# Two 3x3 convolutions by minimal filtering on rows, and a final stage with more buffers

## The chip, the core and the metric

The kernel runs on one core of a Trainium2 chip. The metric is the device time of one execution in microseconds. Before the change it is 2103.16 us (median of three runs, 2087.83 to 2104.97); the profiled execution spans 2096.1 us. Five engines work side by side, each through its own instructions in order: TensorE (PE, with its weight loads as PEld), VectorE (DVE), ScalarE (ACT), GpSimd (POOL), and SyncE (SP), which here issues most DMA transfers.

## What is computed

Two "metaformer" layers on x of shape (2, 256, 56, 56). Layer 0 mixes by 7x7 window attention and then a mixture of eight experts of which each token uses two; layer 1 mixes by two 3x3 convolutions and then another mixture of experts. The change lies in layer 1's convolutions, in what leads into them, and in the last step.

```python
def noised_tri_conv(x, w):
    tw = w - jnp.mean(w)
    tq = ternary_quantize(tw)                 # -1, 0 or 1 by thirds of the range
    out = conv3x3(x, tq)                      # padding 1
    return out + einsum('bchw,oc->bohw', x, tq[:, :, 1, 1])
...
out1 = relu(batch_norm_train(noised_tri_conv(x, w1), g1, b1))
out2 = batch_norm_train(noised_tri_conv(out1, w2), g2, b2)
return relu(out1 + out2)
...
t = t + moe_0(ln(t)); x = x_of(t)
x = x + conv_layer(ln(x)); t = tokens_of(x)
t = t + moe_1(ln(t))
```

The extra term doubles the middle tap, so one convolution with weights of -1, 0, 1 (middle tap -2, 0, 2) gives the whole. The batch norm needs the mean and variance over both images before its first output.

## The kernel before

**Data.** The two images are cut into 14 strips of 8 rows and 56 columns (448 positions); the 256 channels are two halves of 128 partitions (`KC = 2`). `pad[b]` holds one padded image, `X[b, s]` what a convolution gives for one strip, and `XT[b, s]` is the same memory seen as 112 tokens x 4 x 256.

**Order of the stages.** Attention and routing of layer 0; its experts (56 tiles of 256 rows, lines 940 to 1016), which scatter results to `ys`; the two convolutions (`combine`, `split`, `conv`, `affine`, `between`, lines 1532 to 1617); residual, norm and routing of layer 1; its experts; and the final stage (lines 1702 to 1714). In the expert and routing stages the written order is kept on each engine. In the convolutions and the final stage a planner, working from its own idea of costs, orders each engine's instructions; on the chip each engine then keeps that order.

**Weights of the convolutions.** `ternary` (line 1431) makes the quantised weights `wq1` and `wq2` in small steps on VectorE: three reductions for each of nine parts, then three comparisons for each. Two such steps follow each tile of the first experts (`beside`).

**Into the first convolution.** `combine(i)` (line 1532) loads a strip's tokens (`x_on`) and its two expert results per token (`got`, 896 KB, from `ys`, two buffers), adds them with eight multiply-adds on VectorE (line 1058), normalises (`token_norm`, with VectorE doing the scaling, line 1074), turns the strip by TensorE transposes (line 1089), and ScalarE copies it into `pad` (line 1539).

**A convolution.** For each strip, `split` makes two parts of ten rows of `pad`: `hi`, rounded for the fast matmul type (ScalarE, line 1551), and the rest `lo` (VectorE, line 1552), each in two buffers. Then for each output half, 2 input halves x 9 taps x 2 parts = 36 matmuls of 448 columns add into one PSUM block:

```python
for k in range(KC):
    for t in range(TAPS):
        dy, dx = divmod(t, 3)
        for part in (hi, lo):
            nc.tensor.matmul(pc[:, :NT], wq[:, k, t, o * P : (o + 1) * P],
                             part[:, k, dy : dy + SR, dx : dx + W], ...)
```

ScalarE copies the block to `X` (line 1583) and VectorE takes its statistics (line 1584). Between the convolutions `affine` makes scale and shift, and `between` writes the Relu of the scaled result into `pad` on ScalarE (line 1607). GpSimd has nothing to do in either convolution.

**The final stage.** For each strip `gather` loads `got`, adds it to `XT` by eight multiply-adds on VectorE, TensorE turns it, ScalarE copies it to `o_out`, and SyncE stores it. `got` and `o_out` have two buffers each. SyncE issues both loads and stores, in one order.

Of the kernel before, what the change touches and what calls it, by code (L numbers as in the profile page):

```python
# [10 lines left out]
F32 = mybir.dt.float32  # L11
F32R = mybir.dt.float32r
# [8 lines left out]
P = 128  # L21
B, C, H, W = 2, 256, 56, 56
KC = C // P
# [37 lines left out]
TAPS = 9  # L61
NW = C * C * TAPS
# [557 lines left out]
def metaformer(ctx: ExitStack, tc: tile.TileContext, a: dict, out: bass.AP, flag):  # L620
# [427 lines left out]
    def gather(i, ys, wgt, tp, xt):  # L1048

        rows = NTT * TOP * TT  # L1050
        y = tp.tile([TT, NTT, TOP, C], F32, tag="got", name="got")
        nc.sync.dma_start(
            y, ys[i * rows : (i + 1) * rows, :].rearrange("(p t j) c -> p t j c", t=NTT, j=TOP)
        )
        for t in range(NTT):
            n = i * NTT + t
            for j in range(TOP):
                nc.vector.scalar_tensor_tensor(
                    xt[:, t, :], y[:, t, j, :], wgt[:, j, n : n + 1], xt[:, t, :], ALU.mult, ALU.add
                )  # L1060

    def token_norm(tp, xt, eps):
        stats = tp.tile([TT, NTT, 6], F32, tag="t_stats", name="t_stats")
        mv = tp.tile([TT, NTT, 2], F32, tag="t_mv", name="t_mv")
        for t in range(NTT):
            nc.vector.bn_stats(stats[:, t, :], xt[:, t, :])
        for t in range(NTT):
            nc.vector.bn_aggr(mv[:, t, :], stats[:, t, :])
        rstd = tp.tile([TT, NTT], F32, tag="t_rstd", name="t_rstd")
        nc.scalar.activation(rstd, mv[:, :, 1], AF.Sqrt, bias=eps[:TT])  # L1070
        nc.vector.reciprocal(rstd, rstd)
        xn = tp.tile([TT, NTT, C], F32, tag="xn", name="xn")
        for t in range(NTT):
            nc.vector.tensor_scalar(
                xn[:, t, :],
                xt[:, t, :],
                mv[:, t, 0:1],
                rstd[:, t : t + 1],
                ALU.subtract,
                ALU.mult,  # L1080
            )
        return xn
# [17 lines left out]
    def finish(steps):  # L1100
        for _ in steps:
            pass
# [306 lines left out]
    for b, s in STRIPS:  # L1409
        XT[b, s] = xpool.tile([P, NTT, C], F32, tag=f"x{b}_{s}", name=f"x{b}_{s}")  # L1410
        X[b, s] = XT[b, s].rearrange("p t c -> p (t c)")[:, : KC * NT].rearrange(
            "p (k n) -> p k n", n=NT
        )

    with ExitStack() as mid:
# [15 lines left out]
        def ternary(name, wq, ps_pool, tag, tp, held):  # L1431
# [5 lines left out]
            bufs = [t.rearrange("p t c -> p (t c)") for t in held]  # L1437
            wqf = wq.rearrange("p k t c -> p (k t c)")
            parts = [(n, bufs[n // wide][:, n % wide : n % wide + PART]) for n in range(0, size, PART)]

            def load(i):
                n = min(wide, size - i * wide)
                nc.sync.dma_start(bufs[i][:, :n], a[name + "_flat"][:, i * wide : i * wide + n])
# [40 lines left out]
            for n, part in parts:  # L1484
                low = tp.tile([P, PART], F32, tag="low", name="low", bufs=1)
                nc.vector.tensor_scalar(low, part, mean, lo, ALU.subtract, ALU.is_lt)
                yield
                nc.vector.tensor_scalar(part, part, mean, hi, ALU.subtract, ALU.is_gt)
                yield
                nc.vector.tensor_tensor(wqf[:, n : n + PART], part, low, ALU.subtract)  # L1490
                yield
            middle = wq[:, :, TAPS // 2, :]
            nc.vector.tensor_scalar_mul(middle, middle.bitcast(F32), 2.0)
# [3 lines left out]
        wq1 = wqp.tile([P, KC, TAPS, C], F32R, tag="wq1", name="wq1")  # L1497
        wq2 = wqp.tile([P, KC, TAPS, C], F32R, tag="wq2", name="wq2")

        with ExitStack() as st:  # L1500
# [4 lines left out]
            def prepare():  # L1505
                half = len(STRIPS) // 2
                held = [XT[s] for s in STRIPS]
                yield from ternary("L1_conv_w1", wq1, ps, "pt", tp, held[:half])
                yield from ternary("L1_conv_w2", wq2, ps, "pt", tp, held[half:])
# [3 lines left out]
            def beside(j):  # L1513
                for _ in range(2):
                    next(steps, None)
# [6 lines left out]
        with ExitStack() as st:  # L1522
            rp = st.enter_context(tc.tile_pool(name="raw", bufs=1, reuse_waits="tile"))
            tp = st.enter_context(tc.tile_pool(name="conv_t", bufs=2, reuse_waits="tile"))
            ps = st.enter_context(tc.tile_pool(name="conv_ps", bufs=4, space=PSUM, reuse_waits="tile"))

# [5 lines left out]
            def combine(i):  # L1532
                xt = tp.tile([TT, NTT, C], F32, tag="x_on", name="x_on")
                nc.sync.dma_start(xt, x_mid[i])
                gather(i, ys[0], wgt0, tp, xt)
                xn = token_norm(tp, xt, eps6)
# [8 lines left out]
            def split(i):  # L1545

                b, s = STRIPS[i]
                rows = pad[b][:, :, s * SR : s * SR + SR + 2, :]
                hi = tp.tile([P, KC, SR + 2, WC], F32R, tag="hi", name="hi")
                lo = tp.tile([P, KC, SR + 2, WC], F32R, tag="lo", name="lo")  # L1550
                nc.scalar.copy(hi, rows)  # L1551
                nc.vector.tensor_tensor(lo, rows, hi.bitcast(F32), ALU.subtract)  # L1552
                return hi, lo

            def conv(wq, ahead):

                stats = rp.tile([P, KC, len(STRIPS), 6], F32, tag="stats", name="stats")
                ahead(0)
                ahead(1)
                parts = [split(0)]  # L1560
                for i, (b, s) in enumerate(STRIPS):
                    if i + 2 < len(STRIPS):
                        ahead(i + 2)
                    if i + 1 < len(STRIPS):
                        parts.append(split(i + 1))
                    r = X[b, s]
                    hi, lo = parts.pop(0)
                    for o in range(KC):
                        pc = ps.tile([P, 512], F32, tag="cv", name="pc")
                        n = 0  # L1570
                        for k in range(KC):
                            for t in range(TAPS):
                                dy, dx = divmod(t, 3)
                                for part in (hi, lo):
                                    nc.tensor.matmul(  # L1575
                                        pc[:, :NT],
                                        wq[:, k, t, o * P : (o + 1) * P],
                                        part[:, k, dy : dy + SR, dx : dx + W],
                                        start=n == 0,
                                        stop=n == 2 * KC * TAPS - 1,  # L1580
                                    )
                                    n += 1
                        nc.scalar.copy(r[:, o, :], pc[:, :NT])  # L1583
                        nc.vector.bn_stats(stats[:, o, i, :], r[:, o, :])  # L1584
# [16 lines left out]
            stats = conv(wq1, combine)  # L1601
# [13 lines left out]
            stats = conv(wq2, between)  # L1615
# [85 lines left out]
    with ExitStack() as st:  # L1701
        tp = st.enter_context(tc.tile_pool(name="last_t", bufs=2, reuse_waits="tile"))
        ps = st.enter_context(tc.tile_pool(name="last_ps", bufs=2, space=PSUM, reuse_waits="tile"))
        for i, (b, s) in enumerate(STRIPS):
            xt = XT[b, s][:TT]
            gather(i, ys[1], wgt1, tp, xt)
            pu = channels(ps, "pu", xt)
            o = tp.tile([P, KC, NT], F32, tag="out", name="o_out")
# [5 lines left out]
            nc.sync.dma_start(x_out[b, :, :, s * NT : (s + 1) * NT], o)  # L1714
# [116 lines left out]
```

## Time and profile before

| stage | from, us | to, us | length |
|---|---|---|---|
| attention, routing, wait for the first tile | 0 | 673.5 | 673.5 |
| experts of layer 0 | 673.5 | 901.6 | 228.1 |
| until the first convolution's first matmul | 901.6 | 929.9 | 28.3 |
| first convolution | 929.9 | 1154.2 | 224.3 |
| between | 1154.2 | 1161.6 | 7.4 |
| second convolution | 1161.6 | 1376.7 | 215.1 |
| residual and routing of layer 1 | 1376.7 | 1598.3 | 221.6 |
| experts of layer 1 | 1598.3 | 2010.2 | 411.9 |
| final stage | 2010.2 | 2096.1 | 85.9 |

The borders are first and last matmuls of a kind. Over the whole span TensorE is busy 84%, VectorE 39%, ScalarE 31%, GpSimd 28%. A busy TensorE says little by itself, since a matmul's record lasts longer than the distance to the next one; what a matmul costs is that distance. The waits are to be read stage by stage: an engine that is idle in a stage which another one fills costs nothing there.

### The profile page before, as it was taken

To read this page: it belongs to the slowest core of one execution; us is meant where nothing else is said; L and a number is where in the kernel's file an instruction comes from. 1 tells how busy PE (TensorE), PEld (TensorE's weight loads), DVE (VectorE), ACT (ScalarE), POOL (GpSimd) and SP (SyncE) were. 2 spreads that over 40 slices of the span, in tenths; PEclk is the share of its full clock that TensorE was granted. 3 is DMA by queue.
4 is the path that set the end of the run, shared out by engine and by line. 5 is a ranking of instruction groups with operands and counts; after the bars stand their busy time and mean duration, and the time that the engine had idled before them with its cause. 6 is when DMAs were issued, how large, how long until landed. Compare 5 with 4: busy or idle time off the path is not lost. (4 is left out here: it accounts for less than half of the span.)

```text
span 2096.1 us, 27450 instructions
## 1 busy us (share of the span) xinstructions
PE 1750.4 (84%) x9656; PEld 1394.0 (67%) x9656; DVE 819.1 (39%) x2538; ACT 645.6 (31%) x1227; POOL 586.0 (28%) x677
## 2 busy tenths in 40 slices
PE   3999799898882999959999899966435999999953
PEld 1565466464561888848888788855424888888842
DVE  4355345253452656568531111156541111111135
ACT  1444334343241333322211411134312333333311
POOL 4023544334424444510000000015562222222210
PEclk9999899898775999979999999965557999999975
DMA  3000221111114989876310000013325666666647
GB/s 85 28 27 28 63 80 44 55 32 54 59 43 164 316 267 339 287 198 200 97 35 1 0 1 1 1 54 105 99 81 202 230 229 228 229 231 235 224 142 237
DMA packets 77329, 263.48 MB, mean 126 GB/s; under 512 B 16150, under 2 KB 21242, under 8 KB 66880
## 3 DMA queue, kind: packets, MB, share of 16 engines
q1 hardware_dynamic: 55680, 209.83, 31.6%
q0 software_dynamic: 21504, 51.82, 7.1%
q8 instruction: 78, 1.28, 0.3%
q14 instruction: 67, 0.55, 0.1%
HBM read 190.53 MB, written 74.72 MB: 127 GB/s over the span
## 5 line engine op out<-in xcount | busy, mean ns | idle before, releaser
L833 POOL DMA_INDIRECT xs<-u,pos x224 | 215.4, 962 | 623.6 <-ACT ut L748 496.4
L1575 PE MATMUL pc<-hi,wq 128*128 128x448 f32 x1008 | 379.1, 377 | 9.7 <-ACT hi L1551 9.7
L1575 PE MATMUL pc<-lo,wq 128*128 128x448 f32 x1008 | 377.6, 375 | 0.6 <-DVE lo L1552 0.6
L1016 POOL DMA_INDIRECT ys<-y,to x224 | 220.4, 984 | 449.7 <-DVE dest L969 293.3
L990 PE MATMUL ph<-ut,w 128*128 128x256 f32 x1344 | 311.6, 382 | 2.3 <-DMA w<-in_L_experts 2.3
L1006 PE MATMUL py<-w,h 128*128 128x256 f32 x1344 | 308.1, 379 | 1.2 <-DVE y L1014 1.2
L1006 PEld LDWEIGHTS py<-w,h 128*128 128x128 f32 x1344 | 255.3, 190 | 36.2 <-ACT h L997 1.5
L990 PEld LDWEIGHTS ph<-ut,w 128*128 128x128 f32 x1344 | 248.6, 192 | 33.1 <-issue 2.9
L1014 DVE TENSOR_TENSOR y<-py,w 128x512 f32<-128x512 f32 x112 | 77.5, 692 | 426.3 <-PE py L1006 303.8
L1575 PEld LDWEIGHTS pc<-hi,wq 128*128 128x128 f32 x1008 | 192.0, 191 | 32.3 <-ACT hi L1551 10.5
L1575 PEld LDWEIGHTS pc<-lo,wq 128*128 128x128 f32 x1008 | 191.7, 190 | 23.3 <-DVE lo L1552 1.8
L997 ACT ACTIVATE h<-ph,w 128x256 f32<-128x256 f32 x336 | 159.1, 473 | 122.4 <-PE ph L990 97.5
L1257 ACT ACTIVATE ex<-sc 112x476 f32<-112x476 f32 (+3 forms) x224 | 116.8, 571 | 238.9 <-PE sc L1247 188.6
L966 ACT COPY ut<-pt 128x512 f32<-128x512 f32 x112 | 65.6, 586 | 332.3 <-PE pt L962 326.7
L1275 DVE TENSOR_TENSOR acc<-av,acc 128x238 f32<-128x238 f32 (+3 forms) x224 | 89.5, 408 | 168.2 <-PE av L1267 109.3
L1267 PE MATMUL av<-ex,vals 112*64 112x238 f32 (+3 forms) x896 | 127.9, 409 | 7.5 <-DVE acc L1275 5.9
L962 PE MATMUL pt<-ident,xg 128*128 128x128 f32 x448 | 68.8, 278 | 71.8 <-DMA xg<-xs 71.8
L1238 PE MATMUL sc<-q_im,keys 32*112 32x238 f32 (+3 forms) x896 | 108.5, 439 | 20.6 <-issue 15.5
L962 PEld LDWEIGHTS pt<-ident,xg 128*128 128x128 f32 x448 | 57.2, 144 | 82.6 <-DMA xg<-xs 42.1
L1584 DVE BATCH_NORM_STATS2 stats<-x 128x6 f32<-128x448 f32 x56 | 35.0, 625 | 179.1 <-ACT x L1583 178.8
L1583 ACT COPY x<-pc 128x448 f32<-128x448 f32 x56 | 29.7, 531 | 226.2 <-PE pc L1575 226.2
L1267 PEld LDWEIGHTS av<-ex,vals 112*64 112x64 f32 x896 | 58.0, 146 | 59.4 <-issue 32.2
(211 smaller groups left out, 2072.8 us busy)
## 6 DMA issues: line engine op xcount, KB each, us to landing
w<-in_L_experts SPq DMA_DIRECT2D x56, 1154.0 KB
w<-in_L_experts SPq DMA_DIRECT2D x56, 641.0 KB
xg<-xs SPq DMA_DIRECT2D x112, 260.0 KB
got<-ys SPq DMA_DIRECT2D x28, 896.0 KB
xt<-in_x_tok SPq DMA_DIRECT2D x14, 448.0 KB
xr<-in_x_tok SPq DMA_DIRECT2D x14, 448.0 KB
x_mid<-xr SPq DMA_DIRECT2D x14, 448.0 KB
x_on<-x_mid SPq DMA_DIRECT2D x14, 448.0 KB
```

The lines of the kernel that those rows point to most:

```text
L833: w = nc.gpsimd.indirect_dma_start(xs[:, :], bass.IndirectOffsetOnAxis(ap=pos[:, j, t0 + t : t0 + t + 1], axis=0), us[t // NTT][:, t % NTT ...
L962: nc.tensor.transpose(pt[:, k, i * P : (i + 1) * P], d["xg"][:, i, k * P : (k + 1) * P], ident)
L990: nc.tensor.matmul(ph[:, :G], w1[:, k, f * P : (f + 1) * P], d["ut"][:, k, :], start=k == 0, stop=k == KC - 1,)
L997: nc.scalar.activation(d["h"][:, f, :], ph[:, :G], AF.Gelu, bias=b1[:, f : f + 1])
L1006: nc.tensor.matmul(py[:, i, :], d["h"][:, f, i * P : (i + 1) * P], w2[:, f, :], start=f == 0, stop=f == NF - 1,)
L1014: nc.vector.tensor_tensor(y, py, bcast(b2, 1, [P, GP, C]), ALU.add)
L1016: o = nc.gpsimd.indirect_dma_start(ys[:, :], bass.IndirectOffsetOnAxis(ap=d["to"][:, i : i + 1], axis=0), y[:, i, :], None, bounds_check=T ...
L1238: nc.tensor.matmul(sc[h // 2][:, h % 2, :nq], keys[g][p, c, tx * TT : (tx + 1) * TT], q_im[p, c, r0:r1, c0:c1], start=True, stop=False,)
L1257: nc.scalar.activation(e[:, :, :nq], sc[j][:, :, :nq], AF.Exp, scale=HD**-0.5)
L1267: nc.tensor.matmul(av[VW * i : VW * (i + 1), :nq], vals[g % 3][:, tx, 4 * c + 2 * j + i, :], ex[j][:, i, :nq], start=True, stop=True,)
L1275: nc.vector.tensor_tensor(d, av[:, :nq].rearrange("p (h w) -> p h w", w=c1 - c0), d, ALU.add)
L1575: nc.tensor.matmul(pc[:, :NT], wq[:, k, t, o * P : (o + 1) * P], part[:, k, dy : dy + SR, dx : dx + W], start=n == 0, stop=n == 2 * KC * T ...
```

## The change

For two neighbouring output rows of a 3-tap filter (in the row direction), four products replace six. With input rows d0 to d3 and taps g0, g1, g2, the products are (d0 - d2) g0, (d1 + d2)(g0 + g1 + g2)/2, (d2 - d1)(g0 - g1 + g2)/2 and (d1 - d3) g2; the first row is the sum of the first three, the second is the second less the third less the fourth. The three column taps are summed over as before.

- `ternary` now makes the weights of the four products (`sums`, bf16, which holds these small values exactly), six steps more for each input half, and three of its steps follow each expert tile. Before each convolution ScalarE copies `sums` into one `wq`, product by product.
- A unit is two strips (seven units). `component(u, c)` makes input `c` of a unit: `v`, the sum or difference of two rows of `pad` (GpSimd; VectorE in unit 0), then `hi` (ScalarE) and `lo` (VectorE), each of 8 row pairs x 58 columns x 2 halves, in two buffers. The order of the components is 1, 2, 0, 3.
- After a component's matmuls, ScalarE copies (component 1) or VectorE adds and subtracts the PSUM block into the rows of `X`. Statistics are taken after component 3.
- The work for a strip in the first convolution is spread: from strip 3 on, four of the eight multiply-adds become a scaling on ScalarE and an add of 112x1024 on GpSimd; the normalisation's scaling moves from VectorE to ScalarE.
- `X` becomes one tile, so that two strips can be addressed at once.
- In the final stage `got` has eight buffers and `o_out` four, and ScalarE issues the stores.

```diff
-    def gather(i, ys, wgt, tp, xt):
+    def gather(i, ys, wgt, tp, xt, bufs):
+        add_up(i, gathered(i, ys, tp, bufs), wgt, xt, False)
...
+    def add_up(i, y, wgt, xt, apart):
         for t in range(NTT):
             n = i * NTT + t
             for j in range(TOP):
+                g = wgt[:, j, n : n + 1]
+                if apart and j:
+                    nc.scalar.activation(y[:, t, j, :], y[:, t, j, :], AF.Copy, scale=g)
+                else:
                     nc.vector.scalar_tensor_tensor(
+                        xt[:, t, :], y[:, t, j, :], g, xt[:, t, :], ALU.mult, ALU.add
+                    )
+        if apart:
+            nc.gpsimd.tensor_tensor(xt, xt, y[:, :, 1, :], ALU.add)
...
-                nc.vector.tensor_tensor(wqf[:, n : n + PART], part, low, ALU.subtract)
+                nc.vector.tensor_tensor(part, part, low, ALU.subtract)
                 yield
...
+            for k in range(KC):
+                up, mid, down = (g[:, k, y, :] for y in range(3))
+                nc.vector.tensor_copy(sums[:, k, 0, :], up)
+                yield
+                nc.vector.tensor_copy(sums[:, k, 3, :], down)
+                yield
+                nc.vector.tensor_tensor(up, up, down, ALU.add)
+                yield
+                nc.vector.tensor_scalar_mul(mid, mid, 0.5)
+                yield
+                for c, op in ((1, ALU.add), (2, ALU.subtract)):
+                    nc.vector.scalar_tensor_tensor(sums[:, k, c, :], up, 0.5, mid, ALU.mult, op)
+                    yield
...
-                for _ in range(2):
+                for _ in range(3):
                     next(steps, None)
...
-                gather(i, ys[0], wgt0, tp, xt)
-                xn = token_norm(tp, xt, eps6)
+                got = gathered(i, ys[0], tp)
+                add_up(i, got, wgt0, xt, i >= 3)
+                rstd, nmr = finish(token_stats(tp, xt, eps6, True))
+                xn = tp.tile([TT, NTT, C], F32, tag="xn", name="xn")
+                scaled(xn, xt, rstd, nmr)
...
+            def component(u, c):
+                i, j, op = ((0, 2, ALU.subtract), (1, 2, ALU.add), (2, 1, ALU.subtract), (1, 3, ALU.subtract))[c]
...
+                    (nc.gpsimd if u else nc.vector).tensor_tensor(v[:, :, at : at + n, :], *r, op)
+                nc.scalar.copy(hi, v)
+                nc.vector.tensor_tensor(lo, v, hi.bitcast(F32), ALU.subtract)
                 return hi, lo
...
+                order = (1, 2, 0, 3)
+                for c in order:
+                    nc.scalar.copy(wq[:, :, c, :], sums[:, :, c, :])
...
+                for i in range(3):
+                    ahead(i)
+                parts = [component(*steps[n]) for n in range(2)]
+                for n, (u, c) in enumerate(steps):
+                    if n % COMPS == 0:
+                        for i in range(2 * u + 3, min(2 * u + 5, len(STRIPS))):
+                            ahead(i)
+                    if n + 2 < len(steps):
+                        parts.append(component(*steps[n + 2]))
...
                         for k in range(KC):
-                            for t in range(TAPS):
-                                dy, dx = divmod(t, 3)
+                            for dx in range(3):
                                 for part in (hi, lo):
                                     nc.tensor.matmul(
                                         pc[:, :NT],
-                                        wq[:, k, t, o * P : (o + 1) * P],
-                                        part[:, k, dy : dy + SR, dx : dx + W],
+                                        wq[:, k, c, dx * C + o * P : dx * C + (o + 1) * P],
+                                        part[:, k, :, dx : dx + W],
...
-                        nc.scalar.copy(r[:, o, :], pc[:, :NT])
-                        nc.vector.bn_stats(stats[:, o, i, :], r[:, o, :])
...
+                        if c == 1:
+                            nc.scalar.copy(row(1), rows(pc))
+                        elif c == 2:
+                            nc.vector.tensor_tensor(row(0), row(1), rows(pc), ALU.add)
+                            nc.vector.tensor_tensor(row(1), row(1), rows(pc), ALU.subtract)
+                        elif c == 0:
+                            nc.vector.tensor_tensor(row(0), row(0), rows(pc), ALU.add)
+                        else:
+                            nc.vector.tensor_tensor(row(1), row(1), rows(pc), ALU.subtract)
+                            for i in (2 * u, 2 * u + 1):
+                                nc.vector.bn_stats(stats[:, o, i, :], X[STRIPS[i]][:, o, :])
...
-            gather(i, ys[1], wgt1, tp, xt)
+            gather(i, ys[1], wgt1, tp, xt, 8)
             pu = channels(ps, "pu", xt)
-            o = tp.tile([P, KC, NT], F32, tag="out", name="o_out")
+            o = tp.tile([P, KC, NT], F32, tag="out", name="o_out", bufs=4)
...
-            nc.sync.dma_start(x_out[b, :, :, s * NT : (s + 1) * NT], o)
+            nc.scalar.dma_start(x_out[b, :, :, s * NT : (s + 1) * NT], o)
```

## The prediction

> **What bounds the kernel now.** The chain that ended last covers only the final 3 us, so I read the span by stages: the slices of the page (TensorE busy and granted clock) give the borders, the timeline of TensorE sharpens them, and a table of busy times between them tells who is full. Columns: length, then busy time and count on PE, PEld, DVE, ACT, POOL, then granted clock, DMA share, GB/s.
>
> ```profile
> 929.90:1154.20 224.30, 223.99 (x1104) 200.50 (x1104) 107.37 (x287) 44.55 (x76) 0.00 (x0) 0.99 0.31 93
> 1154.20:1161.60 7.40, 0.02 (x1) 0.02 (x1) 1.85 (x7) 5.31 (x9) 0.00 (x0) 0.74 0.00 0
> 1161.60:1376.70 215.10, 214.74 (x1008) 191.71 (x1008) 35.58 (x42) 43.17 (x64) 0.00 (x0) 0.99 0.00 1
> ...
> 2010.20:2096.10 85.90, 28.32 (x112) 16.91 (x112) 45.80 (x113) 13.95 (x28) 1.94 (x2) 0.52 0.76 226
> ```
>
> The convolutions are rows one and three: 439 us, TensorE busy throughout at clock 0.99, the others mostly idle. Only there does fewer matmuls mean less time. The last row is the final stage: no engine is full, DMA is nearest. The groups of the page give the matmuls to be cut:
>
> ```profile
> L1575 PE MATMUL pc<-hi,wq 128*128 128x448 f32 x1008 | 379.1, 377 | 9.7 <-ACT hi L1551 9.7
> L1575 PE MATMUL pc<-lo,wq 128*128 128x448 f32 x1008 | 377.6, 375 | 0.6 <-DVE lo L1552 0.6
> ```
>
> Their 377 ns overlap, so the price is the pitch of starts, which the TensorE timeline shows:
>
> ```profile
> 1153.18 0.37 PE L1575 MATMUL pc<-hi,wq 128*128 128x448 f32 x1
> 1153.39 0.37 PE L1575 MATMUL pc<-lo,wq 128*128 128x448 f32 x1
> 1153.60 0.37 PE L1575 MATMUL pc<-hi,wq 128*128 128x448 f32 x1
> 1153.81 0.37 PE L1575 MATMUL pc<-lo,wq 128*128 128x448 f32 x1
> 1161.58 1.11 PE L1575 MATMUL pc<-hi,wq 128*128 128x448 f32 x2 [7.41 <-ACT hi L1551]
> ```
>
> 0.209 us each: 1008 per convolution are 210.7 us of 224.3 and 215.1. The rest is a cold start (pitch 0.374 for the first 17 matmuls after 1161.6: 2.8 us) and, in the first convolution, the transposes of twelve strips (about 11 us).
>
> [...] VectorE's 112x64 comparison, otherwise 0.22 us, took 1.88 and ended with GpSimd's add (362.27 + 2.35 = 364.62).
>
> ```profile
> 360.88 0.22 DVE L788 TENSOR_TENSOR hot<-order,at 112x64 f32<-112x64 f32 x1
> ...
> 362.82 1.88 DVE L788 TENSOR_TENSOR hot<-order,at 112x64 f32<-112x64 f32 x1
> ```
> ```profile
> 362.27 2.35 POOL L750 TENSOR_TENSOR xr<-xr,u 112x1024 f32<-112x1024 f32 x1
> ```
>
> [...] no run here shows a transfer issued by ScalarE.
>
> **The change part by part.**
>
> *Matmuls.* A unit is two strips; four components, each 2 output halves x 2 input halves x 3 columns x 2 parts = 24 matmuls of the same 448 columns. 7 units x 4 x 24 = 672 for 1008. At 0.209 that is 140.4 for 210.7: 70 us less per convolution, if TensorE stays fed. One component is 5.0 us of TensorE, one unit 20.1; with two strips' transposes 21.7 in the first convolution.
>
> *Feeding it.* Prices: subtraction lo of 928 elements on VectorE 1.12 us (1.366 for 1160, at about 1.06 ns an element); cast hi on ScalarE 0.95 (1.160 for 1160, 0.531 for 448); sum or difference v on GpSimd 2.14 (2.36 for 1024); combination of a PSUM block of 448 0.62 (0.445 for 280, 0.692 for 512); statistics 0.63.
>
> In the first convolution VectorE's unit is 4 lo (4.5) + 8 combinations (5.0) + 4 statistics (2.5) + two strips of expert results at 3.85 each (four of the eight multiply-adds 1.63, token statistics 1.39 + 0.36, three small ones 0.5) = 19.7 us of 21.7. GpSimd gets 4 v (8.6) and two adds of 1024 (4.7) = 13.3. ScalarE has casts 3.8, copies 1.1, pads 2.1, and 16 activations of 256 at up to 0.59: 16.5 at most. Each fits. [...] So I expect blocking[...]: 5.3. VectorE's unit then takes 25 us and, with only two component buffers, sets TensorE's. Behind a blocked lo stand the combinations that free PSUM, and the next strip. Bounds: no blocking gives TensorE's 21.7; 12 us of blocking (each arrival meets a whole operation) gives 32. I take 25 for units 1 to 4; 27 for unit 0 (cold clock; its own v are on VectorE), 22.5 for unit 5 (one strip), 20.5 for unit 6. Sum 170 for 224.3: **-54**.
>
> In the second convolution no strips come: VectorE 12.0, GpSimd 8.6 of 20.1 us. The longest link is cast, wait for a running v, lo: 0.95 + 2.14 + 1.12 = 4.2, under the 5.0 of the component computed meanwhile. So it is TensorE's: 140.4 + cold 2.8 + 1.4 as now = 145. In its first unit casts stand behind up to six Relus (0.67 apart, 4.0 us) on ScalarE: 5 us more. 150 for 215: **-65**.
>
> *Added waits.* A strip's buffers are now freed by GpSimd's add instead of VectorE's; behind that add stand the next v, and behind these the casts of the unit. A late strip therefore stops components that don't need it; I count this in the 25 us and in (c). Keeping the strips in one tile and the weights' sums in bf16 changes addresses and no instruction's length on the path: nothing.
>
> *Start.* The first component needs strips 0 and 1 only, as now, but VectorE's order puts strip 2's eight multiply-adds (data there at 926.6; 3.25), its statistics (1.75), two v (2.24) and small ones ahead of the first lo: ready at 935.6 instead of 929.9: **+6**. The four weight copies (1536 columns, about 1.5 us each) run on ScalarE from 898.8, while expert results are still being waited for until 913.6: nothing.
>
> *Between the convolutions.* Now 7.4. After: combination 0.62, two statistics 1.25, aggregate 0.53, scale and shift 1.6, six Relus 4.0 (halves of strips 0 to 2) instead of four, v 1.12, cast 0.95, hops 0.4: 10.5, **+3**. The next weights are copied component by component once TensorE has left each; only the last is copied in this gap, beside VectorE's statistics. End of the second: one statistic more, **+1**.
>
> *Weight preparation* beside the first experts: three steps per tile for two. VectorE's tile: 0.69 + 0.55 + 3 x 0.68 = 3.3 us of TensorE's 3.89 per tile, so it stays hidden; the twelve extra steps per weight end by tile 44 of 56. Raw weights load faster (2.36 MB in some 35 us for 52), beside DMA at share 0.88; weights are fetched three tiles ahead. I cost it at 0 and keep 4 us for the range.
>
> *Final stage.* Eight buffers for the expert results instead of two, four for the output, the store issued by ScalarE. It moves 14 x 1344 KiB = 19.3 MB in 81.5 us; in its best stretches (2040 to 2050, 2070 to 2080) DMA is 0.97 busy at 285 to 288 GB/s. At that rate 67 us, plus 2 until data flow and 4 after the last (store and end): 73, **-8**. The stores wait on ScalarE for its own copies, which they follow anyway; behind them stand only the next strip's copies. Bounds: -3 (prefetch only shifts the wait to the stores) to -14. VectorE's 45.8 us of work stays below.
>
> Sum: -54 - 65 + 6 + 3 + 1 - 8 = -117 to -118; 2103 - 118 = **1985 us**.
>
> **The rivals.** (a) Forecast, 0.55. (b) TensorE is never starved: first convolution 140.4 + 2.8 + 11 = 154, second 145, final stage -12: 70 + 70 + 12 - 10 = 142, **1961**. For it: TensorE is now full while VectorE takes 107 us, and all sums per unit are below 21.7. Against: the 1.88 us above. 0.23. (c) [...] units of 32 us (27 + 4 x 32 + 27 + 20.5 = 203), second convolution 158, final stage -4: 21 + 57 + 4 - 10 = 72, **2031**. For it: a strip has to pass VectorE, ScalarE, GpSimd, ScalarE and TensorE with two buffers, and even now strips come no faster than one in 7.6 us (nine stores from 916.9 to 978.0), where 10.8 is needed: little slack for a longer way. 0.17. (d) The pauses let the clock fall, as in the routing stage (0.54): 672 x 0.374 = 251, so 262 and 251 us, 74 more than now, + 10 - 8: **2179**, slower. Against: pauses should be of 1 to 2 us. 0.05.
>
> **How the numbers follow.** The range runs from below (b) to above (c), 1950 to 2045, leaving out (d) and the tails of (b) and (c). Slower by over 1% is most of (d), 0.04; within 1% the tails of (c) and (d), 0.02; faster 0.94.
>
> **What would show it.** In the trace of the changed kernel: 1344 matmuls of 448 columns at pitch 0.21; first convolution about 170 us with TensorE idle before matmuls, released by VectorE's lo, and lo longer than 1.12 us beside GpSimd's additions; second about 150 at over 0.95 busy; final stage at DMA share above 0.9. Wrong if lo keeps to 1.12 and TensorE is full (b), if the granted clock in the convolutions is below 0.9 (d), or if the first experts lengthen by over 4 us.

## The result and the profile after

The changed kernel takes 1969.02 us, median of four runs (1961.25 to 1972.59), against 2101.65 us for the kernel before on the same chip (four runs): a ratio of 0.938, 95% interval 0.933 to 0.943. The profiled execution spans 1970.3 us for 2096.1, 125.8 us less. By stages:

| stage | before, us | after, us | difference | forecast |
|---|---|---|---|---|
| attention, routing, first wait | 673.5 | 673.2 | -0.3 | 0 |
| experts of layer 0 | 228.2 | 233.3 | +5.1 | 0, up to +4 |
| until the first convolution | 28.1 | 34.5 | +6.4 | +6 |
| first convolution | 224.3 | 176.9 | -47.4 | -54 |
| between | 7.4 | 8.5 | +1.1 | +3 |
| second convolution | 215.0 | 144.1 | -70.9 | -65 |
| residual and routing of layer 1 | 219.0 | 215.5 | -3.5 | 0 |
| experts of layer 1 | 414.5 | 414.2 | -0.3 | 0 |
| final stage | 86.0 | 70.2 | -15.8 | -8 |

In both columns the experts of layer 1 begin with the transposes of their first tile, at 1595.6 us before the change; the table ahead has that border at 1598.3, hence its 221.6 and 411.9 us. The -3.5 in the routing stage is no effect of the change: that stage measured 215.5, 216.0, 220.4 and 225.5 us in four profiles of kernels that share it. Its last part, the wait for the first expert tile's rows, fell from 42.0 to 37.1 us here.

First the table of busy times by stage, in the columns used in the prediction (length; busy time and count on PE, PEld, DVE, ACT, POOL; clock; DMA share; GB/s). The rows are the experts of layer 0, the start, the two convolutions with the gap between them, and the final stage.

```profile
673.20:906.50 233.30, 224.46 (x1124) 195.28 (x1124) 147.25 (x381) 87.24 (x169) 112.08 (x111) 0.98 0.86 289
906.50:941.00 34.50, 4.23 (x17) 2.31 (x16) 17.91 (x59) 16.39 (x25) 3.19 (x4) 0.55 0.71 195
941.00:1117.90 176.90, 162.93 (x768) 141.16 (x768) 134.07 (x280) 91.32 (x168) 78.77 (x39) 0.94 0.39 111
1117.90:1126.30 8.40, 0.00 (x0) 0.00 (x0) 5.08 (x10) 6.64 (x10) 0.00 (x0) 0.74 0.00 0
1126.30:1270.40 144.10, 144.00 (x672) 128.13 (x672) 82.26 (x113) 47.09 (x63) 49.01 (x28) 0.98 0.00 1
1900.00:1970.30 70.30, 26.89 (x113) 18.19 (x112) 45.80 (x113) 13.92 (x28) 1.95 (x2) 0.53 0.83 276
```

The second convolution is TensorE's from end to end: 144.00 of 144.10 us busy. The first is not: TensorE is idle for 14.0 of 176.9 us, and its granted clock is 0.94. GpSimd, idle there before, now works 78.8 us. The two groups of matmuls have gone from 1008 to 672 each:

```profile
L1604 PE MATMUL pc<-hi,wq 128*128 128x448 f32 x672 | 257.1, 383 | 17.6 <-ACT hi L1575 17.6
...
L1604 PE MATMUL pc<-lo,wq 128*128 128x448 f32 x672 | 256.4, 382 | 0.0
```

TensorE's timeline at the end of the first convolution shows that the pitch is unchanged, 0.21 us from start to start, for 448 columns of the rounded type (the experts' matmuls of 256 columns in plain f32 stand 0.22 us apart in the profile of before: eight in 1.73 us from 689.80):

```profile
1117.07 0.37 PE L1604 MATMUL pc<-lo,wq 128*128 128x448 f32 x1
1117.28 0.37 PE L1604 MATMUL pc<-hi,wq 128*128 128x448 f32 x1
1117.49 0.37 PE L1604 MATMUL pc<-lo,wq 128*128 128x448 f32 x1
1126.35 1.11 PE L1604 MATMUL pc<-hi,wq 128*128 128x448 f32 x2 [8.49 <-ACT hi L1575]
```

Where the first convolution loses time is read from the waits between 941 and 1118 us (engine and what it waited for, total, times, longest): TensorE's, and the top of VectorE's.

```profile
PE pu L1082 <- ACT xn L705: 13.5, 8, 2.8
PE pc L1604 <- ACT hi L1575: 9.1, 1, 9.1
```
```profile
DVE t_stats L684 <- POOL x_on L1075: 14.2, 7, 2.6
DVE lo L1576 <- ACT hi L1575: 11.1, 5, 3.8
```

The 9.1 us is the pause ahead of the first matmul and belongs to the start. Inside the stage TensorE waits eight times, always at a strip's transposes (`pu`), which stand in its order ahead of matmuls that don't need that strip; it never waits for `lo`. VectorE in turn stands 14.2 us before a strip's statistics until GpSimd's addition is done. And the addition holds up VectorE's other work as well: here is one subtraction `lo` on VectorE, and GpSimd's addition beside it.

```profile
1016.41 2.36 DVE L1576 TENSOR_TENSOR lo<-v,hi 128x928 fp32r<-128x928 f32 x1
```
```profile
1015.39 2.40 POOL L1075 TENSOR_TENSOR x_on<-x_on,got 112x1024 f32<-112x1024 f32 x1 [2.85 <-DVE x_on L1071]
```

The addition ends at 1017.79; `lo`, which usually takes 1.12 us, ends 0.98 us after that, as if it had begun only then. It goes the other way too: three of GpSimd's eleven additions in this stage began 0.14 to 0.22 us after a `lo` and took 3.16 to 3.22 us, where the shortest took 2.35.

How much that is can be read from the single durations. In this stage 17 of VectorE's instructions last more than 0.06 us longer than the shortest of their kind, by 17.4 us together. Each of them runs beside an instruction of GpSimd that reads memory, and ends 0.02 to 0.98 us after it: four beside the addition (5.8 us), thirteen beside `v`. Before the change, with GpSimd idle, there is no such instruction in the stage. So the addition costs VectorE less by holding up its other work (5.8 us) than by the waiting for its result (14.2 us).

### The profile page after: what moved, and what is told of

Same layout as the page of the kernel before. It is cut to its first block, busy times and chain, and to the rows that moved or that the text cites. A ratio compares the mean times of both kernels' runs of the same rounds, so it can differ in the third digit from the quotient of the medians.

```text
span 1970.3 us, 26474 instructions
## 1 busy us (share of the span) xinstructions
PE 1625.4 (82%) x8984; PEld 1277.5 (65%) x8984; DVE 913.1 (46%) x2638; ACT 708.9 (36%) x1335; POOL 719.0 (36%) x744
## 5 line engine op out<-in xcount | busy, mean ns | idle before, releaser
L1604 PE MATMUL pc<-hi,wq 128*128 128x448 f32 x672 | 257.1, 383 | 17.6 <-ACT hi L1575 17.6
L1604 PE MATMUL pc<-lo,wq 128*128 128x448 f32 x672 | 256.4, 382 | 0.0
L1574 POOL TENSOR_TENSOR v<-pad 128x928 f32<-128x928 f32 (+1 forms) x56 | 98.4, 1763 | 162.1 <-DVE lo L1576 152.7
L1604 PEld LDWEIGHTS pc<-hi,wq 128*128 128x128 f32 x672 | 129.9, 194 | 33.0 <-ACT hi L1575 18.9
L1604 PEld LDWEIGHTS pc<-lo,wq 128*128 128x128 f32 x672 | 130.4, 194 | 15.1 <-DVE lo L1576 0.7
L964 PE MATMUL pt<-ident,xg 128*128 128x128 f32 x448 | 69.1, 278 | 66.2 <-DMA xg<-xs 65.8
L964 PEld LDWEIGHTS pt<-ident,xg 128*128 128x128 f32 x448 | 57.1, 145 | 77.8 <-DMA xg<-xs 38.0
L1575 ACT CAST hi<-v 128x928 fp32r<-128x928 f32 x56 | 54.0, 965 | 113.4 <-PE pc L1604 107.1
```

The source lines that it names most:

```text
L964: nc.tensor.transpose(pt[:, k, i * P : (i + 1) * P], d["xg"][:, i, k * P : (k + 1) * P], ident)
L1574: (nc.gpsimd if u else nc.vector).tensor_tensor(v[:, :, at : at + n, :], *r, op)
L1604: nc.tensor.matmul(pc[:, :NT], wq[:, k, c, dx * C + o * P : dx * C + (o + 1) * P], part[:, k, :, dx : dx + W], start=m == 0, stop=m == 2 * ...
```

## The experiments

Chips differ: on those of e1 to e8 and of e12 the routing stage of layer 1 takes 179 to 180 us in every profile, and the kernel before 2055 to 2061 us instead of 2102 to 2112. So I compare stages, and ratios only with the kernel before on the same chip. e1 to e9 were executed once each; how far a stage that an edit leaves alone repeats is read from the profiles: the first convolution takes 176.5 to 177.5 us in the five that share it (after, e4, e7, e8, e11), the first experts 232.7 to 236.9 us in the ten after the change that don't have e4's edit. What I call VectorE's excess is worked out from the trace's single durations in the first convolution: for each instruction, its time above the shortest of the same line and shape, summed up. In the changed kernel it is 21.7 us; in the kernel before, 4.4 us, all small scatter.

**e1_store: the strip's store leaves SyncE's queue.**

```diff
                 scaled(xn, xt, rstd, nmr)
+                nc.scalar.dma_start(x_mid[i], xt)
                 pu = channels(ps, "pu", xn)
...
-                nc.sync.dma_start(x_mid[i], xt)
```

> Only the store of the summed strip changes: ScalarE issues it behind its own scaling instead of SyncE ahead of the next loads. Theory A (GpSimd and VectorE exclude each other, VectorE's unit sets the pace): no change, first convolution 175 to 178 us. Theory B (strips come late, because a strip's expert results are loaded only once the strip two ahead has left its buffers, and in SyncE's order also behind the store that waits for GpSimd's add): the buffer frees at the same moment as the store may go, so little, 172 to 176. Theory B' (the order on SyncE alone is the cause): 160 to 165.

Measured: first convolution 186.2 us, excess 29.4. None of the theories. The time got longer by 9 us. Moving the store also changed the planner's orders: VectorE's and TensorE's instructions stand in another order, and GpSimd's additions now hold VectorE up for 13.9 us instead of 5.8. So the order on SyncE alone (B') gets no support, but this run doesn't refute it, since more was changed than that order.

**e2_deep: loads run ahead.** The same, and four places for expert results, up to four for the strip.

```diff
-                xt = tp.tile([TT, NTT, C], F32, tag="x_on", name="x_on")
+                held = {2: 11, 3: 8, 6: 11, 7: 8, 10: 11}.get(i)
...
+                    xt = x_all[:TT, held].rearrange("p (t c) -> p t c", c=C)
...
+                held = {2: 12, 3: 9, 6: 12, 7: 9, 10: 12, 13: 12}.get(i)
...
+                    got = x_all[:TT, held : held + 2].rearrange("p s (t j c) -> p (s t) j c", j=TOP, c=C)
```

> As e1_store, and the strips' tiles get more room in the still empty part of the result tile: four places for expert results, three to four for the strip itself, so loads run ahead. Not one instruction of VectorE or GpSimd is less. Theory A: VectorE's instructions stay 20 us longer than their shortest and the first convolution stays at 170 us or more. Theory B: TensorE's waits for the normalised strip (about 15 us inside the first convolution) nearly vanish; first convolution 155 to 163, whole kernel about 1950 to 1956.

Measured: first convolution 173.6 us, excess 30.9, of which 15.7 us beside the additions; TensorE still waits 10.1 us for the normalised strip. That is theory A's side of the line: with loads ahead the stage stays above 170. It contains e1's edit, though, and is 12.6 us shorter than e1; more room with the store left on SyncE was not tried, so how much late loads cost beside the rest stays open.

**e3_noadd: no addition on GpSimd.**

```diff
-                add_up(i, got, wgt0, xt, i >= 3)
+                add_up(i, got, wgt0, xt, False)
```

> Undoes one part: all eight multiply-adds of a strip on VectorE, as for strips 0 to 2, so no scaling on ScalarE and no addition on GpSimd in the first convolution. VectorE gets 11 x 4 x 0.475 = 21 us more. Theory A: the adds were 2/3 of what blocks, VectorE's excess falls from 22 to about 8 us, and the first convolution takes 165 to 172. Theory B: the chain of a strip loses 2.4 us of addition and a hop and gains 1.9 us: first convolution 172 to 178. If VectorE becomes the bound (152 - 14 + 21 = 159 us of work and idle time as now): 180 to 185.

Measured: first convolution 162.9 us, 14 less than with the change complete, and less than any theory gave; excess 17.6 instead of the 8 that A expected. The row of the busy times for this stage:

```profile
928.80:1091.70 162.90, 157.03 (x768) 135.90 (x768) 145.01 (x323) 76.11 (x127) 50.90 (x28) 0.98 0.40 120
```

VectorE has more to do (145.0 us busy for 134.1), yet is idle only 17.9 us for 42.8. TensorE's longest wait inside the stage is 1.2 us, and its clock is 0.98. So it paid to give VectorE work back. But this run removes two things at once, GpSimd's reading in the addition and two steps in the strip's way (scaling and addition), and the excess hardly fell: beside `v` alone VectorE is held up for 13.1 us now, instead of 11.6. The next two separate them.

**e5_dummy_add and e6_dummy_set: the addition's load without its place in the chain.** Both start from e3_noadd and let GpSimd work on a strip's buffer after VectorE has read it: in e5 it adds (two inputs read), in e6 it writes zeros (nothing read). Nobody uses what they write.

```diff
                 add_up(i, got, wgt0, xt, False)
+                if i >= 3:
+                    nc.gpsimd.tensor_tensor(got[:, :, 0, :], got[:, :, 0, :], got[:, :, 1, :], ALU.add)
```
```diff
                 add_up(i, got, wgt0, xt, False)
+                if i >= 3:
+                    spare = got.rearrange("p t j c -> p (t j c)")
+                    nc.gpsimd.memset(spare, 0.0)
+                    nc.gpsimd.memset(spare[:, :512], 0.0)
```

> As e3_noadd (all multiply-adds on VectorE), but from strip 3 on GpSimd adds the two halves of a strip's expert results into their buffer after VectorE has read them, 112x1024, which nobody uses: the same load of GpSimd and the same hold of that buffer as in the changed kernel, without standing in the strip's chain. Theory A (exclusion of the readers): VectorE's excess rises from 18 to 25 us or more, first convolution from 162.9 to 172-178. Theory G (GpSimd's queue: sums and differences stand behind the additions): 168-176 here and the same in e6. Theory H (what cost the changed kernel is the strip's longer way over ScalarE and GpSimd): 162 to 166.

> As e5_dummy_add, but GpSimd fills the buffer with zeros instead (112x2048 and 112x512, about 2.4 us by the fills in the first stage): as long, at the same place and with the same waits, and reading nothing from memory. Theory A: as e3_noadd, VectorE's excess 16 to 20 us and first convolution 162 to 166. Theory G: as e5. Theory H: 162 to 166, as e5.

The busy times of the first convolution, e5 and then e6:

```profile
930.90:1116.40 185.50, 167.75 (x768) 142.50 (x768) 162.78 (x323) 76.14 (x127) 77.75 (x39) 0.93 0.36 105
```
```profile
931.80:1098.80 167.00, 157.53 (x768) 135.40 (x768) 146.94 (x323) 76.42 (x128) 75.41 (x50) 0.98 0.40 117
```

185.6 us with the adds, 167.0 with the fills, 162.9 with neither; the excess is 36.0, 20.9 and 17.6. GpSimd's load (77.8 and 75.4 us) is nearly the same. TensorE's order is the same in e3, e5 and e6, and VectorE's 323 instructions stand in e5 as in e3, in e6 with one multiply-add moved. What differs is that GpSimd reads: beside the eleven adds VectorE's instructions last 18.6 us longer than their shortest, beside the fills 0.6 us. One place in e5, on VectorE and on GpSimd:

```profile
999.33 2.48 DVE L1071 SCALAR_TENSOR_TENSOR x_on<-got,wgt,x_on 112x256 f32<-112x256 f32 x1
```
```profile
999.16 2.37 POOL L1553 TENSOR_TENSOR got<-got 112x1024 f32<-112x1024 f32 x1 [3.08 <-DVE x_on L1071]
```

A multiply-add of otherwise 0.45 us lasts 2.48: it begins 0.17 us after the addition and ends 0.28 us after it. The eleven adds cost 22.7 us, more than A's 9 to 15, the eleven pairs of fills 4.1 (1 us above A's range). Theory H, by which such adds outside the strip's chain would cost nothing, falls as the whole cause, and so does G, by which both would cost the same. Of e5's 22.7 us some 10 come by way of TensorE's clock: it is busy 167.75 us for 157.03 with the same 768 instructions, at clock 0.93 for 0.98.

**e4_pause: the wait in the weight preparation.**

```diff
             nc.tensor.matmul(pt, ones, st[:, 2:3], start=True, stop=True)
+            for _ in range(9):
+                yield
             mean = tp.tile([P, 1], F32, tag="w_mean", name="w_mean")
```

> In the weight preparation nine empty steps (three expert tiles) go between the cross-partition maximum on GpSimd and its first use on VectorE. Theory C (the first experts are 5 us longer since VectorE stands waiting for that maximum, 8.5 us, with the tile's addition queued behind it and behind three weight steps): first experts 233 to 226-228 us. Theory D (three steps per tile instead of two are too many, 3.3 of 3.89 us): 232 to 234.

Measured: first experts 227.1 us; the first convolution stays at 177.5. Theory C, within its numbers. What VectorE meets is in its timelines, before the change and after:

```profile
742.20 0.16 DVE L1469 TENSOR_TENSOR w_hi<-ext,w_mean 128x1 f32<-128x1 f32 x1 [7.64 <-POOL ext L1460]
...
743.62 0.55 DVE L1486 TENSOR_SCALAR low<-x,w_mean,w_lo 128x512 f32<-128x512 f32 x1
...
744.71 0.69 DVE L1014 TENSOR_TENSOR y<-py,w 128x512 f32<-128x512 f32 x1
```
```profile
728.23 0.16 DVE L1466 TENSOR_TENSOR w_hi<-ext,w_mean 128x1 f32<-128x1 f32 x1 [8.49 <-POOL ext L1457]
...
729.66 0.55 DVE L1483 TENSOR_SCALAR low<-x,w_mean,w_lo 128x512 f32<-128x512 f32 x1
730.24 0.55 DVE L1485 TENSOR_SCALAR x<-x,w_mean,w_hi 128x512 f32<-128x512 f32 x1
730.82 0.69 DVE L1487 TENSOR_TENSOR x<-x,low 128x512 f32<-128x512 f32 x1
...
732.07 0.69 DVE L1016 TENSOR_TENSOR y<-py,w 128x512 f32<-128x512 f32 x1
```

VectorE stands 7.64 and 8.49 us for GpSimd's first maximum over partitions in the two kernels. GpSimd itself is idle for 6.20 and 6.39 us ahead of it, and at the second such maximum VectorE stands only 1.4 and 2.1 us. Before the change one weight step stood between the maximum's arrival and the tile's `y`, which frees TensorE's block: `y` came 2.5 us after `w_hi`. With three steps in a row it came 3.8 us after. TensorE waited 1.2 us before the change and 3.3 after it, and then ran the tile's eight matmuls in 3.57 instead of 1.97 us.

**e7_fin_sync and e8_fin_2: the final stage in halves.** The changed kernel with SyncE's stores again (e7), or with two buffers each again (e8).

```diff
-            nc.scalar.dma_start(x_out[b, :, :, s * NT : (s + 1) * NT], o)
+            nc.sync.dma_start(x_out[b, :, :, s * NT : (s + 1) * NT], o)
```
```diff
-            gather(i, ys[1], wgt1, tp, xt, 8)
+            gather(i, ys[1], wgt1, tp, xt, 2)
-            o = tp.tile([P, KC, NT], F32, tag="out", name="o_out", bufs=4)
+            o = tp.tile([P, KC, NT], F32, tag="out", name="o_out", bufs=2)
```

> The changed kernel with the final stage's stores issued by SyncE again, its buffers kept at eight and four. Theory E (only buffers matter): final stage 69 to 73 us. Theory F (the stores block the loads in SyncE's one order): 77 to 84.

> The changed kernel with two buffers each in the final stage, as before the change, the stores still issued by ScalarE. Theory E: final stage 80 to 85 us. Theory F: 69 to 75.

Measured: 77.2 and 80.8 us, against 86.0 with neither (the profile of before, on another chip) and 67.5 to 71.4 with both (all other runs). So more buffers alone are worth about 9 us, the other queue alone about 5, both about 16: neither theory, each half does its part. In e7 the stores stand between the loads on SyncE and wait there for the copies, 53.0 us for the 14 of them. In e8 SyncE holds loads alone, but twelve of them wait for one of two buffers.

**e9_start: strip 2 behind the first components.**

```diff
-                for i in range(3):
+                for i in range(2):
                     ahead(i)
                 parts = [component(*steps[n]) for n in range(2)]
+                ahead(2)
```

> The changed kernel, except that strip 2 is written behind the first two components of each convolution (only component 3 of the first unit needs its first row). Theory I (VectorE's order, strip 2 ahead of the first lo, makes the start 6 us later): the stretch from the last expert matmul to the first convolution's falls from 34.5 to 28-30 us, the gap between the convolutions from 8.5 to about 7; the first convolution may give 1 to 4 us of it back, since its first unit has the strip's work in it. Theory J (the data or the clock set the start): 33 to 35 us.

Measured: start 29.0 us, as theory I has it, instead of 34.5 (33.1 in e11_again, the changed kernel on the chip of this run); between the convolutions 8.5, unchanged, where theory I had about 7; the first convolution 181.4, 4.5 longer than in the changed kernel's profile and 4.9 longer than in e11_again. On its own chip nothing is left. The work of strip 2 has to be done either way, and from then on it is in the way of the convolution.

**e10_best, e11_again, e12_two: the edits together.** e10_best has the edits of e3, e4 and e9, e12_two those of e3 and e4 alone; e11_again is the changed kernel itself.

> Three edits together: no addition on GpSimd in the first convolution (e3_noadd), the empty steps in the weight preparation (e4_pause), strip 2 behind the first components (e9_start). If they add up: first experts 227 us, start 29, first convolution 163 to 166, second 144, final stage 70, and 22 to 26 us less than the changed kernel on the same chip, about 0.926 of the kernel before. If the second and third meet in VectorE, which e3_noadd shows full in the first convolution: first convolution 168 to 172, 15 to 18 us less.

> The changed kernel itself, on the chip of these runs, so that e10_best has its measure: first convolution 176 to 178 us, start 34.5, first experts 232 to 235, 0.936 to 0.943 of the kernel before.

> e10_best without the edit to the start, which e9_start and e10_best show to be paid back with interest in the first unit: no addition on GpSimd in the first convolution, and the empty steps in the weight preparation. First experts 227 us, start 34.5, first convolution 162 to 165, the rest as in the changed kernel: 20 us less than it, 0.920 to 0.930 of the kernel before. If it falls with e10_best (first convolution 170 or more), it was not the start that made e10_best miss.

| run | first experts | start | first convolution | ratio to the kernel before on its chip |
|---|---|---|---|---|
| e11_again | 233.6 | 33.1 | 176.5 | 0.932 (0.927 to 0.936) |
| e10_best | 227.1 | 30.8 | 172.6 | 0.929 (0.924 to 0.933) |
| e12_two | 225.5 | 35.8 | 162.4 | 0.927 (0.925 to 0.929) |

e10_best falls short of both its forecasts: it is 11 us shorter than e11_again instead of 22 to 26 or 15 to 18, and their intervals overlap, so the two can't be told apart. With the edit to the start, the first unit of the first convolution alone takes 34.5 us (e12_two: 26.3): it takes the gain away. e12_two is the version to keep. Its three stages are 21 us shorter than in the changed kernel's profile, where they sum to 444.7 us. The ratio, 0.927, points the same way, but less clearly: the changed kernel has 0.938 on one chip and 0.932 on another, and it was not executed on the chip of e12_two. The first convolution there:

```profile
922.80:1085.20 162.40, 156.57 (x768) 135.53 (x768) 145.01 (x323) 76.08 (x127) 50.93 (x28) 0.98 0.40 121
```

## Why the prediction was right

The time (1969 for 1985) was right, and so was its main part: a third fewer matmuls at an unchanged pitch, and a TensorE that stays fed in the second convolution. The two convolutions alone are 118.3 of the 125.8 us. That the sum fits so well is luck in part, for several terms were off and their errors cancel. By the profiles the change is worth 125.8 us for the 118 forecast: the first convolution (+7) and the first experts (+5) came out worse, the second convolution (-6), the final stage (-8) and the gap (-2) better, and 3.5 us came from the routing stage. The remaining 8 us of the difference are the runs' own: the medians differ by 132.6 us, the two profiles by 125.8, and the forecast started from 2103.

*Matmuls.* 1344 of 448 columns at pitch 0.21: as predicted.

*First convolution, forecast 170, measured 176.9.* Blocking of VectorE was forecast at 5.3 us a unit. That was my estimate, after one comparison held up in the trace of before, 1.88 us for 0.22. Blocking is there, but smaller: 17.4 us for eleven strips, some 3.2 for each two. The units took 32.1, 25.4, 29.6, 25.9, 23.3, 20.2 and 20.3 us for 27, four times 25, 22.5 and 20.5. The link was named wrongly. The prediction let a blocked `lo` starve TensorE; in fact `lo` is in time (median 1.12 us, and 1.20 in the mean over this stage; two of 28 are held up, for 2.5 us). The rest of the 17.4 us lies in six multiply-adds (6.8 us), in eight small instructions of the strip's normalisation (7.0 us), which the forecast did not count, and in one `v` (1.1 us). What comes late is the normalised strip, whose transposes hold TensorE up in its fixed order. The idle time, 14.0 us, is even less than the 16 that the forecast has above the fed 154. The term that was too small is the clock: I let it be cold once, at the start, and left the rest to rival (d), on the ground that pauses would be of 1 to 2 us. Five of the eight were of 2.1 to 2.8, and after three of them TensorE ran at half clock for 6.1, 3.4 and 3.4 us, half of which, some 6.5 us, is lost. It is busy 162.9 us instead of the fed 154; e3_noadd, cold at its start alone, is busy 157.0. So about 6 of the missing 9 are the clock; the other 3, which e3 has too, I did not trace.

*Second convolution, forecast 150, measured 144.1.* The 5 us for casts behind the Relus did not come: TensorE is busy 144.00 of 144.10 us. Rival (b) had this stage right with 145.

*Added waits.* That a late strip stops components which don't need it was said, and shows: 13.5 us at the transposes, 14.2 us of VectorE behind GpSimd's addition. That it is the addition's reading which costs, e5 and e6 show for e3's arrangement, by 18.6 us between reading and not reading. For the changed kernel it is shown only that leaving out the addition and the scaling with it gains 14 us (e3). How that divides between the 5.8 us for which the addition holds VectorE up and the 14.2 us of waiting for its result isn't shown.

*Start and gap.* Forecast +6 and +3, measured +6.4 and +1.1. e9_start shows that the start has the cause named, VectorE's order. In the gap the six Relus were mis-sized: the first `v` began 2.75 us after the first Relu, behind four of them, not the 4.0 us of all six.

*Weight preparation, forecast 0, up to 4, measured +5.1.* The step failed, and one of the prediction's own signs of being wrong, first experts longer by over 4 us, came true. The sum of VectorE's work per tile (3.3 of 3.89 us) was right, but the preparation has one place where VectorE stands still, and I counted none. e4_pause and e12_two show it: with the wait filled, 227.1 and 225.5 us.

*Final stage, forecast -8, bounds -3 to -14, measured -15.8.* The direction was right, the price wrong. Counted from the first load, the stage took 81.5 us before the change, was forecast at 73 and took 65.8; a DMA share above 0.9, as forecast, it has from 1905 to 1955 us, but not over its whole length (0.83). I took 288 GB/s, the best stretches of the final stage before at a DMA share of 0.97, for what a full DMA moves. The stretches of the changed kernel say otherwise; the first line is from before the change:

```profile
2040.00:2050.00 10.00, 4.04 (x16) 2.43 (x16) 5.60 (x14) 2.94 (x6) 0.00 (x0) 0.50 0.97 288
```
```profile
1905.00:1915.00 10.00, 2.06 (x8) 1.15 (x8) 4.13 (x11) 0.29 (x1) 0.00 (x0) 0.50 0.98 253
1915.00:1925.00 10.00, 6.12 (x24) 3.74 (x24) 9.69 (x26) 2.84 (x7) 0.00 (x0) 0.50 1.02 300
1925.00:1935.00 10.00, 5.84 (x24) 3.80 (x24) 8.88 (x23) 3.22 (x7) 0.00 (x0) 0.50 1.03 372
1935.00:1945.00 10.00, 4.05 (x16) 2.44 (x16) 8.61 (x22) 1.82 (x5) 0.00 (x0) 0.50 1.02 365
```

At the same share of about 1.0 it moves 253 GB/s while only loads run, and 365 to 372 later, with stores among them. The mix of loads and stores alone doesn't explain that: stores are a third of the bytes before the change too (2025 to 2085 us, 274 GB/s), and in e7, with eight buffers and the stores on SyncE:

```profile
1885.00:1925.00 40.00, 18.14 (x72) 10.84 (x72) 29.54 (x73) 8.71 (x19) 0.00 (x0) 0.50 0.97 312
```

What differs is how long a load's packet of 8 KB takes: 468 ns on average in that stretch before the change, 418 in this one of e7, 355 in the changed kernel from 1925 to 1955 us. In these runs the highest rate came only with more buffers and the second issuing engine together: e8, with two buffers, has 285 GB/s from 1875 to 1920 us. The forecast gave the second issuing engine no bandwidth of its own, which no run had shown then. With eight buffers it was 312 GB/s with one and 365 to 372 with two; whether the engine itself does it or the loads that no longer stand behind stores on SyncE isn't shown, nor why the packets take less time. The trace of before had a warning that I did not use: a stretch of the first experts at share 0.98 and 356 GB/s.

```profile
790.00:810.00 20.00, 20.00 (x104) 17.45 (x103) 12.53 (x32) 7.97 (x16) 10.09 (x11) 1.00 0.98 356
```

*Rivals.* (b) gave 1961, nearer to the time than the forecast, with the wrong first convolution (154) and the right second. (c) is refuted as a whole, 176.9 for 203, though engines held up by each other's fixed orders, which it counted on, show in TensorE's 13.5 us at the transposes. (d) is refuted as a state, but appears in small, as the 6 us above.

## What to carry to other kernels

Work taken off VectorE and put on GpSimd was no relief here, where both read memory at the same time and VectorE had to wait for the result: price what is held up (17.4 us of VectorE's time here) and the wait (14.2 us) before the sum of busy times. A step that "fits beside" another needs its longest wait looked up, not only its total, and what stands behind that wait. A DMA share near 1 doesn't say how much is moved (253 to 372 GB/s here): a forecast from the rate of one stretch needs a wide range, even where the mix of loads and stores stays the same.

## What was unexpected in the hardware

TensorE lost its full clock after short pauses, and their length alone doesn't tell after which. In the first convolution of the two profiles of the changed kernel, pauses of 2.82, 2.41, 2.13, 2.84, 2.03 and 2.10 us were followed by half clock, pauses of 2.22, 2.33 and 2.22 us were not, and none of 1.8 us or less was; in e5_dummy_add two of 1.81 and 1.83 us were. One of them on TensorE's timeline; a matmul's record lasts 0.57 us at half clock, 0.37 at full.

```profile
1005.86 0.63 PE L1082 MATMUL pu<-ident,xn 112*128 112x112 f32 x2 [2.41 <-ACT xn L705]
...
1007.47 0.57 PE L1604 MATMUL pc<-lo,wq 128*128 128x448 f32 x1
...
1009.33 0.37 PE L1604 MATMUL pc<-hi,wq 128*128 128x448 f32 x1
```

The recorded clock shows more. In the profiles of the kernel before and of the changed kernel its changes all lie a whole number of times 3.41 us apart. Here is the changed kernel in such stretches, around the pause of 2.41 us and around one of 2.33 (length, then TensorE's busy time; the clock is third from the end):

```profile
1002.41:1005.82 3.41, 1.04 (x5) 0.59 (x4) 2.76 (x6) 2.66 (x7) 2.82 (x2) 1.00 0.00 0
1005.82:1009.24 3.42, 3.38 (x13) 2.93 (x14) 1.67 (x8) 2.33 (x5) 1.71 (x1) 0.50 0.30 79
...
1022.89:1026.30 3.41, 2.24 (x11) 1.67 (x9) 3.41 (x7) 0.29 (x1) 2.57 (x2) 1.00 0.24 60
1026.30:1029.71 3.41, 2.17 (x13) 1.78 (x14) 2.00 (x5) 3.41 (x8) 2.36 (x1) 1.00 0.07 23
1029.71:1033.12 3.41, 3.41 (x20) 3.04 (x19) 3.37 (x11) 2.30 (x7) 2.02 (x2) 1.00 0.92 268
```

The pause of 2.41 us falls into one stretch, TensorE is busy for 1.04 us of it, and the next stretch runs at half clock. The pause of 2.33 us is cut in two by a border, and the clock stays. In the first convolutions of all fourteen profiles, 661 such stretches at full clock, the clock fell after 32: in them TensorE was busy for at most 1.69 us, in one for 2.04. It stayed after the other 629, all with 1.57 us or more. In the changed kernel's own first convolution it fell after three, with 1.04 to 1.28 us of work, for the next 3.41, 3.41 and 6.83 us, and stayed after 42, all with 1.91 us or more. Outside this stage busy time doesn't tell them apart: in the profile of before, TensorE was busy for all of the 3.41 us from 355.61, at full clock, and the next 3.41 us ran at 0.50.

Small instructions were held up as well: VectorE's product of two 112x4 operands, 0.15 us at its shortest in the first convolution, took up to 1.60 us and 0.48 in the mean, and one of these stands in the way of each strip. So was one with a single input from memory: the change of sign of 112x4 values ahead of it (`t_nmr<-t_mv`) took up to 1.71 us for 0.15, four times of eleven, and ended 0.02 to 0.03 us after a `v` of GpSimd each time.
